# Expert weights in another order: second weights four rows to a partition, first weights read with a stride

## The chip, the cores and the metric

The kernel runs on one core of one Trainium2 chip. The metric is the device time of one execution in microseconds (us). The kernel before takes 616.64 us, the median of 9 runs between 615.38 and 618.8 us. The numbers on single instructions come from one profiled execution, which took 621.12 us.

## What is computed

Two transformer layers on `x` of 8 x 512 x 128 values in 32-bit floating point. Layer 0 is an attention with linear state plus a mixture of 8 experts of one matrix each. Layer 1 is an attention with a local window and latents plus a mixture of 8 experts with two matrices each. The part that the change touches is the expert layer of layer 1:

```python
logits = x_flat @ gate_w.T
probs = jax.nn.softmax(logits / TEMPERATURE, axis=-1)
topk_probs, topk_idx = jax.lax.top_k(probs, TOPK)          # 2 of 8
hidden = jax.nn.relu(jnp.einsum('th,ehf->tef', x_flat, w1) + b1[None])
all_out = jnp.einsum('tef,efh->teh', hidden, w2) + b2[None]
gathered = jnp.take_along_axis(all_out, topk_idx[:, :, None], axis=1)
y_flat = jnp.sum(gathered * topk_probs[:, :, None], axis=1)
```

`w1` is 8 x 128 x 512 and `w2` is 8 x 512 x 128. The kernel computes only the two chosen experts of each token. The sum over the 512 hidden units in the second product may be taken in any order, so long as both matrices and the bias `b1` agree on which unit is which.

## The kernel before

The 8 sequences form three groups of 2, 3 and 3. After layer 0, each group goes through `route` (L1152), `experts1` (L1309) and, in parallel with it, `attention1` (L923); `output` (L1431) adds the two. `route` sorts the tokens of a group by expert into tiles of 128 rows, so that each tile has one expert: 85 tiles in all.

For each tile, `fetch` (L1316) issues three loads on the queue of SyncE (SP): `load_first` (L1336), the first weights of the tile's expert, 128 partitions of 512 values; `load_second` (L1340), the second weights, with the hidden unit `k*128 + p` on partition p, block k; and `load_third` (L1344), the output bias spread over the partitions. Loads run three tiles ahead, in 3 buffers of first weights, 4 of second weights and 4 of bias. The expert's number is read into SP's registers (L1323). On TensorE (PE), `hp` (L1405 to 1410) is then made by four products of 128x128 by 128x128, one for each block k of 128 hidden units; the block of first weights is the stationary operand (it is loaded into the array), the tokens are the moving one. ScalarE (ACT) applies bias and relu into `ht`, and four more products add up into `yp` (L1420 to 1425), with `ht` stationary and the block k of second weights moving. In the profile each 32-bit product is two weight loads (PEld) and two matmuls (PE).

The first bias `b1` comes with the packed weights as columns. At the start it is transposed into `b1r` (L608 to 610): 32 rows of 128 values, row `4*e + k` holding the units of block k of expert e. `route` picks rows out of it by a product with a one-hot matrix `ohk` (L1226 to 1233), built from two constants that say which expert (`part4`, L109) and which block (`chunk4`, L110) a row of `b1r` belongs to. Its result is the tile's bias, used by the relu of L1414.

The order of all instructions is not written by hand. A recorder (L126) keeps every operation with its engine and an estimated time (`_duration`), and `order` (L238) lays them out with a list scheduler, by readiness and by the ranks of a table `PLAN` (L1461). The instructions are then emitted in that order, and each engine runs its own in that order. Operations recorded that way all show the line 389 in the profile; only the loads of `fetch` and the scatter L1371 have lines of their own. For a matmul, the estimate looks at the shapes of the operands and not at their strides. Where the plan has PE idle, `_fill` (L349) puts matmuls on zeros. SP's queue carries, besides the expert weights, the store of each sequence's layer-0 gates to memory (`gd`), the loads that spread them over the partitions (`gbc`, L704), the token rows, and the final reads and stores.

Of the kernel before, what the change touches and what calls it, by code (L numbers as in the profile page):

```python
# [10 lines left out]
F32 = mybir.dt.float32  # L11
# [8 lines left out]
P = 128  # L20
# [3 lines left out]
E = 8  # L24
FF = 512
NFC = FF // P
# [11 lines left out]
def _tiles(n):  # L38
    return (2 * n * N + E * (P - 1)) // P
# [34 lines left out]
def _constants():  # L74

    c = np.zeros((P, _CN), np.float32)
    p = np.arange(P)

    def put(name, a):
        lo, hi = _CCOL[name]  # L80
        c[: a.shape[0], lo:hi] = a.reshape(a.shape[0], hi - lo)

    put("ident", np.eye(P))

    less = np.eye(P)
    less[P - 1] = -1.0
    less[:, P - 1] = 0.0
    put("less", less)
    put("heads", p[:, None] // D == p[None, :] // D)
    put("head4", (p[:, None] // D) % 4 == np.arange(4)[None, :])  # L90
    put("head8", (p % LC)[:, None] // D == np.arange(LH)[None, :])

    i = np.arange(W)[None, :]
    put("seen_q", i <= p[:, None] % W)
    put("seen_k", p[:, None] % W <= i)
    put("past_k", p[:, None] % W > i)

    g = np.arange(P // CHUNK)
    late = np.zeros((P, P), np.float32)
    group = np.zeros((P, P), np.float32)  # L100
    for at in (0, LC):
        late[at : at + len(g)] = np.where(p[None, :] % len(g) > g[:, None], NEG, 0.0)
        group[at : at + len(g)] = p[None, :] // CHUNK == g[:, None]
    put("late", late)
    put("group", group)
    put("first", np.broadcast_to(E - np.arange(E), (P, NT, E)))
    put("before", p[:, None] < p[None, :])
    put("iota", np.broadcast_to(p, (P, P)))
    put("part4", p[:, None] // NFC)  # L109
    put("chunk4", p[:, None] % NFC == np.arange(NFC)[None, :])  # L110
    put("within", p)
    n = 2 * max(GROUPS) * NT
    put("tile", np.broadcast_to(1 + np.arange(n), (P, n)))
    return c
# [321 lines left out]
def two_layers_kernel(  # L436
# [14 lines left out]
    nc = Recorder(tc.nc)  # L451
# [5 lines left out]
    work = ctx.enter_context(tc.tile_pool(name="work", bufs=2))  # L457
    small = ctx.enter_context(tc.tile_pool(name="small", bufs=2))
    dram = ctx.enter_context(tc.tile_pool(name="dram", bufs=4, space=DRAM))
# [52 lines left out]
    def wt(name):  # L512
        lo, hi = _WCOL[name]
        return wsb[:, lo:hi]
# [62 lines left out]
    nc.gpsimd.memset(vb, 0.0)  # L577


    b1r = const.tile([E * NFC, P], F32, name="b1r")  # L580

    def mm(o, lhsT, rhs, start=True, stop=True):
        nc.tensor.matmul(o, lhsT, rhs, start=start, stop=stop)

    def bank(name, parts=P):
        t = ps.tile([parts, 512], F32, tag="bank", name=name)
        nc.banks[t[:].tensor.name] = t[:]
        return t
# [18 lines left out]
    less_last(wk0, wsb[:, lo : lo + kq], bias_row("k"), "k0", plus=3)  # L607
    b1p = bank("b1p")  # L608
    nc.tensor.transpose(b1p[: E * NFC, :P], wt("b1"), ident)
    nc.scalar.copy(b1r, b1p[: E * NFC, :P])  # L610

    def layernorm(dst, src, name, n=C):

# [695 lines left out]
    def experts1(h):  # L1309

        nm = f"_{h}"
        TILES = _tiles(GROUPS[h])
        row_i, token_i, _, bias, own_i = places[h]
        ws, xgs, xts, hts, numbers = {}, {}, {}, {}, {}

        def fetch(j):  # L1316

            if j % QUAD == 0:
                n = min(QUAD, TILES - j)
                number = own_i[0:1, j : j + n]  # L1320

                def load(q=j // QUAD):
                    _, numbers[q] = tc.nc.values_load_multi_w_load_instructions(  # L1323
                        number, engines=(mybir.EngineType.SP,), min_val=0, max_val=E - 1,
                        skip_runtime_bounds_check_because="a count of experts, held under E on the chip",
                    )

                nc.add("SP", load, [], [number], 1.5, 0.0)
                fetch.last = nc.ops[-1]
            first = work.tile([P, FF], F32, tag="w1", name=f"w1{nm}_{j}", bufs=3)  # L1330
            second = work.tile([P, NFC, C], F32, tag="w2", name=f"w2{nm}_{j}", bufs=4)
            third = work.tile([P, C], F32, tag="b2", name=f"b2{nm}_{j}", bufs=4)

            def load_first():
                e = bass.ds(numbers[j // QUAD][j % QUAD], 1)
                tc.nc.sync.dma_start(first, w1[e].rearrange("e p f -> (e p) f"))  # L1336

            def load_second():
                e = bass.ds(numbers[j // QUAD][j % QUAD], 1)
                tc.nc.sync.dma_start(second, w2[e].rearrange("e (k p) c -> p (e k) c", p=P))  # L1340

            def load_third():
                e = bass.ds(numbers[j // QUAD][j % QUAD], 1)
                tc.nc.sync.dma_start(third, experts_b[e, 1].to_broadcast([P, C]))  # L1344

            for move, to in ((load_first, first), (load_second, second), (load_third, third)):
                nc.add("SP", move, [to], [], 0.55, 3.3)
                nc.ops[-1].follows = (fetch.last,)
            ws[j] = first, second, third

        def gather(q):
            js = range(q * QUAD, min((q + 1) * QUAD, TILES))
            if not len(js):
                return
            xg = work.tile([P, QUAD, C], F32, tag="xgt", name=f"xgt{nm}_{q}", bufs=2)
            for a, j in enumerate(js):
                nc.gpsimd.indirect_dma_start(
                    xg[:, a], None, x_rows[h],
                    bass.IndirectOffsetOnAxis(ap=token_i[:, j : j + 1], axis=0),
                )  # L1360
            xgs[q] = xg

        views = dram_disjoint_views(y_rows[h], TILES)
        scattered[h] = []

        def scatter(j, ys):

            ids = row_i[:, j : j + 1]

            def store():  # L1370
                tc.nc.gpsimd.indirect_dma_start(  # L1371
                    views[j], bass.IndirectOffsetOnAxis(ap=ids, axis=0), ys, None
                )

            nc.add("POOL", store, [], [ys, ids], 1.25, 2.4)
            scattered[h].append(nc.ops[-1])

        def turn(q):
            if q not in xgs:
                return  # L1380
            xg = xgs.pop(q)
            n = min(QUAD, TILES - q * QUAD)
            tp = bank(f"tpx{nm}_{q}")
            for a in range(n):
                nc.tensor.transpose(tp[:, a * P : (a + 1) * P], xg[:, a], ident)
            xt = work.tile([P, QUAD * P], F32, tag="xt", name=f"xt{nm}_{q}", bufs=2)
            nc.scalar.copy(xt[:, : n * P], tp[:, : n * P])
            xts[q] = xt

        for j in range(AHEAD):  # L1390
            fetch(j)
        gather(0)
        yield
        turn(0)
        gather(1)
        yield
        for j in range(TILES + 1):
            if j < TILES:
                if j + AHEAD < TILES:
                    fetch(j + AHEAD)  # L1400
                q, a = divmod(j, QUAD)
                if a == 1:
                    turn(q + 1)
                    gather(q + 2)
                hp = bank(f"hp{nm}_{j}")  # L1405
                for k in range(NFC):
                    mm(
                        hp[:, k * P : (k + 1) * P], ws[j][0][:, k * P : (k + 1) * P],
                        xts[q][:, a * P : (a + 1) * P],
                    )  # L1410
                ht = work.tile([P, NFC, P], F32, tag="ht", name=f"ht{nm}_{j}", bufs=2)
                for k in range(NFC):
                    nc.scalar.activation(
                        ht[:, k], hp[:, k * P : (k + 1) * P], AF.Relu, bias=bias[:, k, j : j + 1]  # L1414
                    )
                hts[j] = ht
                yield
            if j:
                ht, (_, w2k, b2) = hts.pop(j - 1), ws.pop(j - 1)
                yp = bank(f"yp{nm}_{j - 1}")  # L1420
                for k in range(NFC):
                    mm(
                        yp[:, :C], ht[:, k], w2k[:, k],
                        start=k == 0, stop=k == NFC - 1,
                    )
                ys = work.tile([P, C], F32, tag="ys", name=f"ys{nm}_{j - 1}", bufs=YS)
                nc.vector.tensor_add(ys, yp[:, :C], b2)
                scatter(j - 1, ys)
                yield
# [49 lines left out]
    def put(name, stage, arg, at):  # L1479
        nc.begin(*PLAN[name][at])  # L1480
        for _ in stage(arg):
            pass
# [73 lines left out]
```

## Time and profile before

| what | value |
|---|---|
| median of 9 runs | 616.64 us |
| profiled execution | 621.12 us, of which 619.1 us from first to last instruction |
| mean granted TensorE clock | 0.961 of full speed |
| experts' first product, weight loads | 680, mean 194 ns, 186 at least |
| experts' first product, matmuls | 680, mean 280 ns, from 131.1 us to 579.7 us of the span |
| loads of second weights (L1340) | 85, issue 384 ns in the median |
| loads of first weights (L1336) | 85, issue 333 ns in the median |
| DMA queue of SP and ACT (q1) | 100,582 packets, 78.41 MB, 43.9% of 16 engines' span |

The span is the time from the first to the last instruction; the 2 us that the execution lasts beyond it are the start and the end around it. "Busy" is the time in which an engine has an instruction under way. Matmuls are pipelined: one of 275 ns overlaps the next, so the distance from start to start, not the duration, tells what a matmul costs in a row of matmuls. PEld is the loading of the stationary operand, which goes on beside the matmul of the operand loaded before.

### The profile page before, as it was taken

The page shows a single profiled execution, that of the slowest core. Times are in us where ns is not written, and L with a number is a line of the kernel's source. Part 1 is how long each engine was busy: PE and PEld are TensorE (multiplying, and loading weights), DVE is VectorE, ACT ScalarE, POOL GpSimd, SP SyncE. Part 2 cuts the span into 40 slices and gives each one's busy share as a digit, 9 for nine tenths or more (in the row PEclk, how much of TensorE's full clock was granted, in tenths as well). Part 3 has the DMA queues.
Part 4 walks back from the last instruction along what each step waited for, and adds up shares of the span by engine and source line. Part 5 has one row for each costly group of instructions (what it writes and reads, how often), then busy time and mean ns, then how long its engine had stood idle before and what let it go on. Part 6 is the DMA issues. An engine that isn't in the chain of part 4 may idle for free.

```text
span 619.1 us, 15660 instructions
## 1 busy us (share of the span) xinstructions
PE 550.7 (89%) x5487; PEld 453.9 (73%) x5487; DVE 477.0 (77%) x1297; ACT 342.7 (55%) x950; POOL 403.4 (65%) x422
## 2 busy tenths in 40 slices
PE   9999988889989899869998979988998899999873
PEld 3567766669778678758897867987777788888832
DVE  2396899988979889998867867789844784965695
ACT  2532746761864784536577347464485567557610
POOL 3015323679748837864777877887778888887562
PEclk8799999978999999999998889989999999999996
DMA  5035142554442334636654466666956767796222
GB/s 158 1 115 143 52 128 74 152 143 133 116 132 78 107 112 130 138 68 181 186 164 140 138 188 209 175 176 193 254 179 194 226 207 232 208 264 200 71 86 69
DMA packets 106532, 91.63 MB, mean 148 GB/s; under 512 B 8940, under 2 KB 84086, under 8 KB 106454
## 3 DMA queue, kind: packets, MB, share of 16 engines
q1 hardware_dynamic: 100582, 78.41, 43.9%
q0 software_dynamic: 5440, 11.15, 7.0%
q10 hardware_dynamic: 432, 1.07, 0.5%
q8 instruction: 44, 0.72, 0.5%
q14 instruction: 34, 0.28, 0.2%
HBM read 80.70 MB, written 9.90 MB: 146 GB/s over the span
## 4 chain that ended last, share of the span: by engine, by line
DVE 33%; PE 27%; POOL 15%; issue 8%; ACT 8%; DMA 8%; SPq 0%; DVEq 0%; POOLq 0%; ACTq 0%
PE rp L389 4%; POOL m L389 4%; PE hp L389 4%; DVE pw L389 4%; PE yp L389 3%; POOL y_rows L1371 3%; DMA gbc<-gd 3%; PE pv L389 3%; POOL xgt L389 2%; POOL pw L389 2%; ACT vb L389 2%; DVE m L389 2%; DMA xgt<-x_rows,token_i 2%; DVE xg L389 2%; DVE x L389 2%
## 5 line engine op out<-in xcount | busy, mean ns | idle before, releaser
L389 ACT ACTIVATE ht<-hp,bias 128x128 f32<-128x128 f32 x340 | 101.2, 372 | 44.8 <-PE hp L389 44.5
L1371 POOL DMA_INDIRECT y_rows<-ys,row_i x85 | 89.4, 1052 | 42.4 <-issue 9.7
L389 POOL DMA_INDIRECT xgt<-x_rows,token_i x85 | 87.2, 1026 | 23.0 <-issue 17.3
L389 PEld LDWEIGHTS hp<-xt,w 128*128 128x128 f32 x680 | 84.2, 194 | 12.8 <-issue 5.3
L389 PE MATMUL hp<-xt,w 128*128 128x128 f32 x680 | 91.7, 280 | 2.0 <-DVE ys L389 1.0
L389 PE MATMUL yp<-w,ht 128*128 128x128 f32 x680 | 90.6, 278 | 1.4 <-ACT ht L389 1.4
L389 PEld LDWEIGHTS yp<-w,ht 128*128 128x128 f32 x680 | 83.1, 192 | 6.6 <-ACT ht L389 3.0
L389 PE MATMUL rp<-we_sb,xg 128*128 128x128 f32 x512 | 68.2, 281 | 6.0 <-POOL xg L389 3.7
L389 POOL TENSOR_TENSOR xg<-xT,gbc 128x512 f32<-128x512 f32 x32 | 43.2, 1350 | 43.9 <-DMA gbc<-gd 31.3
L389 PEld LDWEIGHTS rp<-we_sb,xg 128*128 128x128 f32 x512 | 62.7, 195 | 11.8 <-POOL xg L389 6.5
L389 PE MATMUL pv<-pw,vb 128*32 128x64 f32 (+1 forms) x1088 | 37.9, 229 | 18.2 <-POOL pw L389 13.0
L389 PEld LDWEIGHTS pv<-pw,vb 128*32 128x32 f32 x1088 | 34.4, 119 | 25.3 <-POOL pw L389 22.1
L389 ACT ACTIVATE m<-m,zero_b 128x512 f32<-128x512 f32 x32 | 23.1, 723 | 39.6 <-POOL m L389 39.4
L389 POOL TENSOR_TENSOR pw<-pt,csb 128x512 f32<-128x512 f32 x32 | 42.3, 1323 | 3.6 <-DVE pt L389 3.3
L389 POOL TENSOR_TENSOR m<-m,ard 128x512 f32<-128x512 f32 x32 | 34.1, 1066 | 12.0 <-DVE ard L389 5.1
L389 DVE TENSOR_TENSOR pw<-pt,csb 128x512 f32<-128x512 f32 x32 | 40.5, 1267 | 0.3
L389 POOL TENSOR_TENSOR m<-m,amx 128x512 f32<-128x512 f32 x32 | 33.8, 1065 | 10.7 <-DVE amx L389 9.8
L389 POOL TENSOR_TENSOR le<-le,lrd 128x128 f32<-128x128 f32 (+3 forms) x32 | 23.9, 753 | 25.9 <-DVE lrd L389 18.7
L389 ACT COPY vb<-v 32x128 f32<-32x128 f32 x128 | 37.7, 295 | 1.8
L389 DVE COPY_PREDICATED m<-csb,sc 128x256 f32<-128x256 int32 x64 | 25.3, 435 | 15.3 <-POOL m L389 12.0
L389 PE MATMUL sc<-kT,qe 32*128 32x64 f32 x1024 | 36.0, 277 | 1.0 <-DVE k L389 0.6
L389 PEld LDWEIGHTS sc<-kT,qe 32*128 32x128 f32 x1024 | 33.0, 190 | 4.4 <-DVE k L389 1.1
(261 smaller groups left out, 1221.0 us busy)
## 6 DMA issues: line engine op xcount, KB each, us to landing
w<-in_w_dram SPq DMA_DIRECT2D x170, 256.0 KB
gbc<-gd SPq DMA_DIRECT2D x64, 256.0 KB
b<-in_experts_b_dram SPq DMA_DIRECT2D x85, 64.0 KB
yg<-y_rows SPq DMA_DIRECT2D x16, 256.0 KB
x<-in_x_dram SPq DMA_DIRECT2D x8, 256.0 KB
x_rows<-xn SPq DMA_DIRECT2D x8, 256.0 KB
out_dram<-x SPq DMA_DIRECT2D x8, 256.0 KB
xgt<-x_rows,token_i POOLq DMA_INDIRECT x85
```

Of the source, the lines that this page charges most:

```text
L389: r.ENGINES[name], lambda: call(*args, **kwargs), aps[:1], aps[1:], time, delay, shape
L1371: tc.nc.gpsimd.indirect_dma_start(views[j], bass.IndirectOffsetOnAxis(ap=ids, axis=0), ys, None)
```

## The change

The second weights are laid out so that partition p holds the hidden units `4*p` to `4*p + 3`. These four rows of `w2` lie next to each other in memory, so that one partition's data is one piece of 2 KB, where it was four pieces of 512 bytes. Block k is then the units `4*p + k`, so the first product takes, for block k, every fourth column of the first weights, beginning with k: a stride of 16 bytes in the stationary operand. The bytes moved are the same, and so are the number and shape of the products.

The bias has to follow. `b1r` now has the row `8*k + e`, holding the units `4*p + k` of expert e. At the start the transposed bias goes to a temporary tile `b1t`, from there by a store of 16 KB to a scratch in memory `b1d`, and comes back by four loads of 8 rows of 128 single values each (every fourth value). The two constants `part4` and `chunk4` are changed to the new row order. The five added DMAs are issued on SP's queue.

```diff
-    put("part4", p[:, None] // NFC)
-    put("chunk4", p[:, None] % NFC == np.arange(NFC)[None, :])
+    put("part4", p[:, None] % E)
+    put("chunk4", p[:, None] // E == np.arange(NFC)[None, :])
...
     nc.tensor.transpose(b1p[: E * NFC, :P], wt("b1"), ident)
-    nc.scalar.copy(b1r, b1p[: E * NFC, :P])
+    b1t = work.tile([E * NFC, P], F32, tag="pt", name="b1t", bufs=1)
+    nc.scalar.copy(b1t, b1p[: E * NFC, :P])
+    b1d = dram.tile([E, FF], F32, tag="b1d", name="b1d", bufs=1)
+    nc.sync.dma_start(b1d.rearrange("e (c p) -> (e c) p", p=P), b1t)
+    for k in range(NFC):
+        nc.sync.dma_start(
+            b1r[k * E : (k + 1) * E], b1d.rearrange("e (p k) -> k e p", k=NFC)[k]
+        )
...
-                tc.nc.sync.dma_start(second, w2[e].rearrange("e (k p) c -> p (e k) c", p=P))
+                tc.nc.sync.dma_start(second, w2[e].rearrange("e (p k) c -> p (e k) c", k=NFC))
...
                     mm(
-                        hp[:, k * P : (k + 1) * P], ws[j][0][:, k * P : (k + 1) * P],
+                        hp[:, k * P : (k + 1) * P], ws[j][0][:, k::NFC],
                         xts[q][:, a * P : (a + 1) * P],
                     )
```

## The prediction

> **What bounds the kernel now.** I read the page's busy shares first, then the chain that ended last, then the windows of the expert stage, all instructions and `hp` alone.
>
> ```profile
> PE 550.7 (89%) x5487; PEld 453.9 (73%) x5487; DVE 477.0 (77%) x1297; ACT 342.7 (55%) x950; POOL 403.4 (65%) x422
> ...
> DVE 33%; PE 27%; POOL 15%; issue 8%; ACT 8%; DMA 8%; SPq 0%; DVEq 0%; POOLq 0%; ACTq 0%
> PE rp L389 4%; POOL m L389 4%; PE hp L389 4%; DVE pw L389 4%; PE yp L389 3%; POOL y_rows L1371 3%; DMA gbc<-gd 3%; PE pv L389 3%; POOL xgt L389 2%; POOL pw L389 2%; ACT vb L389 2%; DVE m L389 2%; DMA xgt<-x_rows,token_i 2%; DVE xg L389 2%; DVE x L389 2%
> ```
>
> PE is the fullest engine, but the chain passes from one engine to another: PE holds 27% of it, and `hp` alone 3.6% (the chain's own view gives the tenths), 22.3 us of 619.1. DMA holds 8%, and the weights hardly appear. In the waits, PE and PEld wait for the weights `w` 1.6 us in all. SP's queue waits far longer for PE to free weight buffers (64.4 us at L1340) than anyone waits for the loads. So the transfer that the change improves is hidden now, and the weight load that it alters is on the fullest engine.
>
> The windows from 130 to 582 us, where all 680 passes of `hp` lie (a pass is one weight load with its matmul). Columns: stretch and its length, PE busy (count), PEld busy (count); in the second view of `hp` alone.
>
> ```profile
> 130.00:200.00 70.00, 63.49 (x667) 54.37 (x666) 60.49 (x157) 39.19 (x104) 53.58 (x53) 0.98 0.45 129
> 200.00:290.00 90.00, 78.90 (x848) 65.25 (x849) 84.40 (x241) 57.20 (x152) 58.03 (x58) 1.00 0.43 114
> ...
> 430.00:500.00 70.00, 63.70 (x639) 53.77 (x638) 46.34 (x122) 41.26 (x127) 56.65 (x60) 1.00 0.73 210
> 500.00:582.00 82.00, 78.20 (x913) 69.81 (x912) 52.39 (x120) 54.57 (x172) 63.83 (x66) 1.00 0.73 208
> ```
>
> ```profile
> 130.00:200.00 70.00, 6.36 (x48) 5.83 (x48) 7.26 (x24) 0.98 0.45 129
> 200.00:290.00 90.00, 11.72 (x88) 10.92 (x88) 12.81 (x42) 1.00 0.43 114
> ...
> 430.00:500.00 70.00, 20.32 (x152) 18.53 (x152) 21.48 (x75) 1.00 0.73 210
> 500.00:582.00 82.00, 24.57 (x184) 22.63 (x184) 27.93 (x98) 1.00 0.73 208
> ```
>
> PE is idle there for 6.5, 11.1, 4.2, 8.1, 6.3 and 3.8 us (the two stretches left out have 72 and 136 passes): 40 us of 452, and least where `hp` is densest.
>
> **Part 1, the strided weight load.** First, what sets the pace of a pass. The timeline of PEld at 98.6 us shows weight loads beside short matmuls; that of 340 us shows one tile's `hp`:
>
> ```profile
> 98.64 0.30 PEld L389 LDWEIGHTS cp<-m,csb 128*128 128x128 f32 x2
> 98.86 0.30 PEld L389 LDWEIGHTS tot<-m,ones 128*128 128x128 f32 x2
> 99.08 0.30 PEld L389 LDWEIGHTS wgp<-wgl,wqT 128*128 128x128 f32 x2
> ```
>
> ```profile
> 340.09 0.97 PEld L389 LDWEIGHTS hp<-xt,w 128*128 128x128 f32 x8
> ```
>
> `cp` and `tot` have matmuls of only 64 moving columns, and still their loads follow each other at 0.22/2 = 110 ns. So a load of 128 columns in 32-bit takes 110 to 112 ns of the array's time by itself. `hp` runs at (0.97 - 0.19)/7 = 111 ns per pass; I use 112. A matmul of 128 columns needs nearly the same (the gate transposes `gp`, with a weight of 8 columns, follow at 109 ns in the trace's records). The two streams are level, so whatever the load loses, the pass loses: there is no slack to hide a slower load.
>
> No weight load of the trace has a stride; the memory patterns recorded for them are all contiguous. The bounds on a load with a stride of 16 bytes:
> - From below: 112 ns, no change. A gain is excluded, since the matmul holds the pass at 109 ns (at most 3 ns x 680 = 2 us).
> - From above: the 128 values now lie over 2,048 bytes of the partition, where they lay over 512. If the read had to walk the whole stretch at today's rate, 4 x 112 = 448 ns, +336 ns x 680 = 228 us.
> - Between: the fastest weight read of the trace is that of `ohr` in 16 bits, 256 bytes in (0.40 - 0.19)/7 = 30 ns (eight `inv` matmuls in 0.40 us, each 0.19). Walking 2,048 bytes at that rate takes 240 ns. I take a doubling, 224 ns: next to that row, and the geometric middle of 112 and 448. Extra: 112 ns x 680 = 76 us of PE time.
>
> [...]
>
> How much of 76 us reaches the end? By stage the extra is 48, 88, 72, 136, 152 and 184 passes x 0.112 = 5.4, 9.9, 8.1, 15.2, 17.0 and 20.6 us. Bounds: nothing absorbed, 76. The present chain lengthened only by its own `hp` pieces, doubled: 22. Between them, all of PE's idle time taken up stage by stage: 0 + 0 + 3.9 + 7.1 + 10.7 + 16.8 = 38.5. I take the middle of 22 and 76, 49 us. What is late next is ACT, which waits for `hp` already (44.5 us in 35 waits), then `ht`, `yp` and the scatter.
>
> **Part 2, second weights in pieces of 2 KB.** Per load 128 packets instead of 512, the same bytes. In the trace's packet records one of 512 bytes takes 28.8 ns in the mean (75,016 packets), one of 2,048 bytes 109.5 ns (median 84; 19,136 packets). On each of 16 engines a load goes from 32 x 28.8 = 0.92 us to 8 x 109.5 = 0.88, or 8 x 84 = 0.67 at best: 0.04 to 0.25 us less. PE waits for `w` 1.6 us in all, so the direct gain is at most that. Behind the loads in the queues, `gbc`, `xgt` and the bias land sooner; the chain has 8% = 50 us of landings in some 20 pieces, so at most 20 x 0.25 = 5 us. I take 1 us. SP's issue falls from 384 ns to the 333 of L1336, 4 us of an engine that is not on the chain: nothing.
>
> **Part 3, the bias at the start.** The copy on ACT (0.25 us) stays. The store is as large as `gd`'s (0.33 us issue; landing 1.45 us in the chain). Four loads of 1,024 single values: the trace's two loads of 128 single values took 0.55 us to issue against 0.28 for a plain one, 2.1 ns a value, so some 2.5 us each, and their packets 9 ns. On 8 engines 4,096 packets take 4.6 us, on one 37. From 16.7 us (copy done) this gives about 29 us for the issue. SP has nothing between 9.1 and 32.05 us (`gd`), and `b1r` is first read at 107.1 us: nothing, covered by that gap. If the cover fails, the gates of the first sequence come late by up to 25 us at the very worst (16.7 + 3 + 37 = 57 against 32); I keep 0 to 5. The wait that `bp` gains is long satisfied. `b1t` borrows a buffer whose next user starts at 119.2 us. The recorder's estimate sees no stride, so the order of the other engines should stay.
>
> **Sum.** Profiled execution: 621.1 + 49 - 1 = 669. The median of the runs is 4.5 us below the profiled one: 616.6 + 48 = 664.6, said as 665.
>
> **The rivals.**
> 1. The strided load is as fast as the contiguous one. For: nothing in the trace says that the array's own 112 ns isn't what bounds a load. Against: the 16-bit row shows that the array takes weights faster, so 112 is a rate of reading. Then only parts 2 and 3 remain: 616.6 - 1 = 615.6, between 611.6 and 617.8. This is the case on the other side: shorter landings of `gbc` and `xgt` behind the weight loads, at the end of the expert stage where DMA is busy 0.73, pay from the point at which the load costs under 1 us / 680 = 1.5 ns more.
> 2. A partial price, 1.2 to 1.6 times: 22 to 67 ns x 680 = 15 to 46 us of PE time, of which two thirds (49/76) arrive: 626 to 646.
> 3. The walk at today's rate, 448 ns: +228 us, less the idle 40: about 805.
>
> **How the numbers follow.** Doubled (638 to 692 by the bounds 22 and 76): 0.46. No price: 0.36. Partial: 0.13. Quadrupled: 0.03. A late start or a changed order that outweighs the rest: 0.02. The doubled case's own range is 638 to 692. With two cases so far apart, the range runs from within the free case to within the doubled one: 613.5 to 685; it leaves out some 0.05 of the free case, 0.06 of the doubled one and the 0.03. About 0.2% (1.2 us) is what a measurement of this kernel can tell from no change. Within the free case 615.4 is about the middle: faster 0.17, same 0.17, slower by the rest 0.66.
>
> **What would show it.** PEld rows of `hp`: mean near 300 ns instead of 194, eight of them over 1.7 us instead of 0.97; `yp` beside it unchanged at 192. PE idle in the windows after 350 us nearly gone. If the `hp` loads stay at 194, part 1 is wrong and the time is near 615.6. If they double and the time grows by under 22 us, the path was misread. The weights' packets should fall by 32,640, and SP's queue should stand free before `gd` at 32 us.

## The result, and the profile after

The changed kernel takes 648.25 us in the median (644.97 to 651.75, 15 runs), the kernel before beside it 616.51 us (46 runs). The ratio is 1.0516, 95% interval 1.0498 to 1.0534: 31.7 us slower. The profiled execution of the changed kernel has a span of 651.6 us.

The page of the changed kernel shows the busy shares, the chain that ended last by engine and by line, and the groups of the first product, of its relu and of the second product's weight loads:

```profile
PE 613.7 (94%) x5487; PEld 526.2 (81%) x5487; DVE 478.6 (73%) x1297; ACT 345.5 (53%) x950; POOL 402.7 (62%) x422
...
PE 67%; DVE 19%; POOL 4%; ACT 4%; DMA 3%; issue 2%; SPq 0%; DVEq 0%; POOLq 0%
PE hp L389 23%; PE yp L389 11%; PE rp L389 5%; PE pv L389 4%; PE sc L389 3%; PE kp L389 2%; PE rem_p L389 2%; PE gj L389 2%; DVE xg L389 2%; DVE pw L389 2%; DMA gbc<-gd 2%; PE sl L389 1%; POOL m L389 1%; DVE x L389 1%; PE tpx L389 1%
...
L389 PEld LDWEIGHTS hp<-xt,w 128*128 128x128 f32 x680 | 165.5, 327 | 8.7 <-issue 2.6
L389 PE MATMUL hp<-xt,w 128*128 128x128 f32 x680 | 171.0, 397 | 0.3 <-ACT gsb L389 0.3
L389 ACT ACTIVATE ht<-hp,bias 128x128 f32<-128x128 f32 x340 | 101.8, 368 | 98.7 <-PE hp L389 96.7
...
L389 PEld LDWEIGHTS yp<-w,ht 128*128 128x128 f32 x680 | 82.8, 192 | 4.1 <-issue 2.4
```

PE now holds 67% of the chain, where it held 27%, and `hp` alone 23%. The weight load of `hp` went from 194 to 327 ns in the mean; that of `yp`, which reads its block contiguously, stayed at 192. No other engine's busy time moved by more than 3 us. ACT's waits for `hp` doubled, from 44.5 to 96.7 us, but ACT has only 4% of the chain, and PE waits for its `ht` 0.5 us in all.

The windows of the changed kernel, columns as in the prediction, the last one 32 us longer because the experts end later:

```profile
130.00:200.00 70.00, 66.99 (x675) 58.92 (x674) 60.77 (x161) 39.72 (x104) 54.04 (x54) 1.00 0.46 130
200.00:290.00 90.00, 84.11 (x832) 72.55 (x831) 83.64 (x236) 56.21 (x149) 57.33 (x57) 1.00 0.40 111
...
430.00:500.00 70.00, 69.81 (x542) 64.00 (x541) 42.07 (x119) 36.87 (x114) 51.07 (x53) 1.00 0.64 182
500.00:614.00 114.00, 114.00 (x1107) 105.96 (x1106) 63.27 (x146) 62.72 (x192) 76.22 (x77) 1.00 0.64 177
```

From 430 us on PE is idle for 0.2 us in all (70 - 69.81, then 114 - 114.00); in the kernel before it was idle for 6.3 and 3.8 us in the last two windows. The pace of a pass is read from the timeline of PEld, two tiles in a row:

```profile
548.96 3.81 PEld L389 LDWEIGHTS hp<-xt,w 128*128 128x128 f32 x16
```

(3.81 - 0.33)/15 = 232 ns from load to load, where it was 111. In the trace's records the median is 233 ns against 111 to 112: about 121.5 ns more for each of 680 passes, 82.6 us of PE time. Of that, 31.7 us (38%) arrived. In both traces PE runs its 5,487 matmuls in the same order, so the difference does not come from another schedule. The open questions were two: whether the load alone is to blame, and where the other 51 us went.

### The profile page after: what moved, and what is told of

Its sections match the earlier page's. It is cut to its first block, busy times and chain, and to the rows that moved or that the text cites. A ratio compares the mean times of both kernels' runs of the same rounds, so it can differ in the third digit from the quotient of the medians.

```text
span 651.6 us, 15669 instructions
## 1 busy us (share of the span) xinstructions
PE 613.7 (94%) x5487; PEld 526.2 (81%) x5487; DVE 478.6 (73%) x1297; ACT 345.5 (53%) x950; POOL 402.7 (62%) x422
## 4 chain that ended last, share of the span: by engine, by line
PE 67%; DVE 19%; POOL 4%; ACT 4%; DMA 3%; issue 2%; SPq 0%; DVEq 0%; POOLq 0%
PE hp L389 23%; PE yp L389 11%; PE rp L389 5%; PE pv L389 4%; PE sc L389 3%; PE kp L389 2%; PE rem_p L389 2%; PE gj L389 2%; DVE xg L389 2%; DVE pw L389 2%; DMA gbc<-gd 2%; PE sl L389 1%; POOL m L389 1%; DVE x L389 1%; PE tpx L389 1%
## 5 line engine op out<-in xcount | busy, mean ns | idle before, releaser
L389 PEld LDWEIGHTS hp<-xt,w 128*128 128x128 f32 x680 | 165.5, 327 | 8.7 <-issue 2.6
L389 PE MATMUL hp<-xt,w 128*128 128x128 f32 x680 | 171.0, 397 | 0.3 <-ACT gsb L389 0.3
L389 ACT ACTIVATE ht<-hp,bias 128x128 f32<-128x128 f32 x340 | 101.8, 368 | 98.7 <-PE hp L389 96.7
L389 PE MATMUL yp<-w,ht 128*128 128x128 f32 x680 | 89.0, 276 | 0.0
L389 DVE TENSOR_TENSOR ys<-yp,b 128x128 f32<-128x128 f32 x85 | 24.0, 283 | 37.7 <-PE yp L389 37.4
L389 PEld LDWEIGHTS pv<-pw,vb 128*32 128x32 f32 x1088 | 31.2, 112 | 14.2 <-POOL pw L389 10.5
L389 PE MATMUL pv<-pw,vb 128*32 128x64 f32 (+1 forms) x1088 | 34.6, 219 | 8.1 <-POOL pw L389 5.6
```

The costliest lines, as they stand in the source:

```text
L389: r.ENGINES[name], lambda: call(*args, **kwargs), aps[:1], aps[1:], time, delay, shape
```

## The experiments

All runs but the last one below (the second dose) were made on a chip on which the kernel before takes about 642 us; so each run is compared with the kernel before of its own series, and times are given as ratios. In the runs marked with "columns" the products take other columns than the reference's, as the expectations say; the work is of the same size.

**Theory 1**: the strided weight load is the whole cause, and packets and bias detour cost and bring nothing. **Rival**: one of these has a part in the loss.

### Stride alone (columns)

```diff
-                        hp[:, k * P : (k + 1) * P], ws[j][0][:, k * P : (k + 1) * P],
+                        hp[:, k * P : (k + 1) * P], ws[j][0][:, k::NFC],
```

The edit is made in the kernel before.

> The kernel before with one edit: the first weights are read with the stride of 16 bytes; second weights and bias stay in the old order, so the hidden units of the two products do not agree (that part of the computation is changed). Theory 1, the strided weight load is the whole cause: the changed kernel's time, 649 us (647 to 651), hp loads of 329 ns. Rival, the new layout of the second weights or the bias detour has a part in the loss: at most 640 us.

Measured: ratio 1.051 (1.044 to 1.058), the changed kernel's 1.0516 within its interval; 674.09 us on that chip, so the absolute time of the expectation does not apply. The loads have a median of 329 ns. The stride alone gives the whole loss.

### Everything but the stride (columns)

```diff
-                        hp[:, k * P : (k + 1) * P], ws[j][0][:, k::NFC],
+                        hp[:, k * P : (k + 1) * P], ws[j][0][:, k * P : (k + 1) * P],
```

The edit is made in the changed kernel.

> The changed kernel with the first weights read in contiguous blocks again; 2 KB pieces of second weights and the bias detour stay, so the hidden units of the two products do not agree (that part is changed). Theory 1: the kernel before less what the bigger packets bring, 615.5 us (613.5 to 617). Rival, packets or detour cost by themselves: 620 us or more.

Measured: ratio 1.0009 (0.9976 to 1.0043). The rival falls. The loads have a median of 192 ns again. Packets of 2 KB and the detour together change nothing that can be measured; a gain of over 0.24% is excluded. Two things in the traces fit this: PE waited for the weights 1.6 us in all, and the bigger packets are hardly faster (in the changed kernel 30,016 packets of 2,048 bytes take 109.6 ns in the mean, four of 512 bytes took 4 x 28.8 = 115). The run doesn't tell the two apart.

### Two rows to a partition: stride of 8 bytes

```diff
-                tc.nc.sync.dma_start(second, w2[e].rearrange("e (p k) c -> p (e k) c", k=NFC))
+                tc.nc.sync.dma_start(second.rearrange("p (h d) c -> p h (d c)", d=2), w2[e].rearrange("e (h p d) c -> p (e h) (d c)", h=2, d=2))
...
-                        hp[:, k * P : (k + 1) * P], ws[j][0][:, k::NFC],
+                        hp[:, k * P : (k + 1) * P], ws[j][0][:, k // 2 * 2 * P + k % 2 : k // 2 * 2 * P + 2 * P : 2],
```

The edit is made in the changed kernel. The bias detour is rearranged in the same way (not shown), so both products agree on the units.

> Two rows of second weights to a piece of 1 KB, so the first weights are read with a stride of 8 bytes. Theory 1a, the load slows only when no two neighbours lie within 16 bytes: loads of 192 ns, time 616 us (614 to 617.5). Theory 1b, the price grows with the stretch walked (16 bytes cost 122 ns a pass, 8 bytes a third of the way from 1 to 4, 40 ns, 27 us of PE time): loads near 235 ns, time 624 to 632 us.

Measured: ratio 1.0024 (0.9987 to 1.0062); loads of 196 ns, 118 ns from load to load instead of 112. Nearly theory 1a: a stride of 8 bytes costs 6 ns a pass and not 40. No gain shows in it either.

### Strides of 1, 2, 3 and 4 in one kernel (columns)

```diff
-                hp = bank(f"hp{nm}_{j}")
+                step = 1 + j % 4
+                hp = bank(f"hp{'abcd'[j % 4]}{nm}_{j}")
...
-                        hp[:, k * P : (k + 1) * P], ws[j][0][:, k * P : (k + 1) * P],
+                        hp[:, k * P : (k + 1) * P], ws[j][0][:, k * (P if step == 1 else 1) :][:, : step * (P - 1) + 1 : step],
```

> The kernel before with strides of 1, 2, 3 and 4 values in the first weights of every fourth tile (hpa, hpb, hpc, hpd); the first product takes other columns than it should in three tiles of four. Theory 1a (two values within 16 bytes suffice): loads of 192, 192, then 192 to 260 for 12 bytes, and 329 ns. Theory 1b (price grows with the stretch): 192, 235, 280 and 329 ns. Time between before and after, 620 to 632 us.

The loads by tile (columns: count, then shortest, median and longest duration in ns, then first and last start):

```profile
L389 PEld LDWEIGHTS hpa<-xt,w x176: 186/192/333, 127.3 to 596.0; 128*128 128x128 f32 x176
...
L389 PEld LDWEIGHTS hpb<-xt,w x176: 193/197/332, 128.9 to 598.1; 128*128 128x128 f32 x176
...
L389 PEld LDWEIGHTS hpc<-xt,w x176: 251/262/333, 132.6 to 602.7; 128*128 128x128 f32 x176
...
L389 PEld LDWEIGHTS hpd<-xt,w x152: 308/329/332, 148.0 to 591.2; 128*128 128x128 f32 x152
```

The medians are 192, 197, 262 and 329 ns, and the paces in the records 112, 118, 174 and 233 ns. Neither theory gave all four: 8 bytes are almost free (1a), but from there on the pace grows by 56 to 59 ns for each value of stride (1b). Two readings remain: a fixed price per piece of 16 bytes touched (64, 96 and 128 pieces at strides 2, 3 and 4: 1.84, 1.81 and 1.82 ns a piece), or a price per byte of the stretch walked. The kernel was run once: 643.37 us, against 642.12 in the median for the kernel before, below the 620 to 632 us of the expectation (0.6 to 2.5% over the kernel before) although the slower loads add some 30 us of PE time. One run has no interval, so this only hints at what "Where the rest of the 82.6 us went" tests.

### Strides of 4, 5, 6 and 8 (columns)

```diff
-                hp = bank(f"hp{nm}_{j}")
+                step = (4, 5, 6, 8)[j % 4]
+                hp = bank(f"hp{'abcd'[j % 4]}{nm}_{j}")
...
-                        hp[:, k * P : (k + 1) * P], ws[j][0][:, k * P : (k + 1) * P],
+                        hp[:, k * P : (k + 1) * P], we_sb.rearrange("p e c -> p (e c)")[:, k : k + step * (P - 1) + 1 : step],
```

> The kernel before, with the stationary operand of the first product taken out of the 1,024 columns of layer 0's expert weights at strides of 4, 5, 6 and 8 values (hpa, hpb, hpc, hpd by every fourth tile); the first product is therefore another one. Theory L, the price is one unit per piece of 16 bytes touched, and a stride over 16 bytes touches no more pieces than values: pitch 233 ns at 4, 5, 6 and 8 alike. Theory S, the price goes with the stretch of memory walked (8.8 bytes per ns, as strides 2, 3 and 4 have it): 233, 291, 350 and 466 ns.

```profile
L389 PEld LDWEIGHTS hpa<-xt,we_sb x176: 307/329/333, 130.8 to 625.8; 128*128 128x128 f32 x176
...
L389 PEld LDWEIGHTS hpb<-xt,we_sb x176: 294/314/338, 132.6 to 628.6; 128*128 128x128 f32 x176
...
L389 PEld LDWEIGHTS hpc<-xt,we_sb x176: 296/316/340, 137.1 to 634.1; 128*128 128x128 f32 x176
...
L389 PEld LDWEIGHTS hpd<-xt,we_sb x152: 312/334/338, 152.1 to 620.2; 128*128 128x128 f32 x152
```

The paces are 233, 220, 222 and 237 ns. Theory S (up to 466) falls and theory L holds within 6%: the times go with the pieces of 16 bytes that the load touches, 1.7 to 1.9 ns each, and from a stride of 16 bytes on it touches one piece per value and gets hardly worse (233 ns at 16 bytes, 237 at 32). Another size of piece does not fit: pieces of 8 bytes would make strides of 8 and 16 bytes alike, where 118 and 233 ns were measured, and pieces of 32 would make 32 bytes twice as dear as 16. That strides of 5 and 6 are 5% faster than 4 and 8 was not expected, and is left open.

### Where the rest of the 82.6 us went

**Theory A**: PE's own waiting swallowed it, so that the first part of the extra work is cheap and the last is paid in full. **Theory B**: a constant share, 39% as I put it, arrives, as of any work of which a part lies on the chain.

In the changed kernel, with `early` as `h < 2`, `late` as `h == 2` and `half` as `j % 2` (columns in all three):

```diff
-                        hp[:, k * P : (k + 1) * P], ws[j][0][:, k::NFC],
+                        hp[:, k * P : (k + 1) * P], (ws[j][0][:, k::NFC] if early else ws[j][0][:, k * P : (k + 1) * P]),
```

> The changed kernel with the strided load only in the first two groups (54 tiles, 432 passes); the third group reads contiguous blocks, so its two products disagree on the hidden units (that part is changed). Extra weight-load time 432 x 0.1215 = 52.5 us. Theory A, the extra is paid out of the time in which TensorE would have waited anyway, and little of that is left at the end: of the 5.1% this carries 1.2 to 2.4%, ratio to the kernel before 1.012 to 1.024. Theory B, a constant share (39%) of the extra arrives wherever it lies: 1.032.

> The changed kernel with the strided load only in the third group (31 tiles, 248 passes); the first two groups read contiguous blocks, so their two products disagree on the hidden units (that part is changed). Extra 248 x 0.1215 = 30.1 us. Theory A: most of it arrives, ratio 1.025 to 1.035, more than from the early groups although the extra is smaller. Theory B: 1.018.

> The changed kernel with the strided load in every second tile (41 of 85, 328 passes); the other tiles read contiguous blocks, so their two products disagree on the hidden units (that part is changed). Extra 39.9 us, spread evenly. Theory A, the first part of an even extra is nearly free and the last part costs in full: ratio 1.004 to 1.016, less than half of 1.051. Theory B: half of it, 1.025.

| where the stride is | extra on PE | ratio to before, interval | A | B |
|---|---|---|---|---|
| groups 1 and 2 | 52.5 us | 1.0273, 1.0218 to 1.0329 | 1.012 to 1.024 | 1.032 |
| group 3 | 30.1 us | 1.0237, 1.0171 to 1.0302 | 1.025 to 1.035 | 1.018 |
| every second tile | 39.9 us | 1.0103, 1.0039 to 1.0166 | 1.004 to 1.016 | 1.025 |

The two runs by group lie between the theories and decide nothing: the measured ratios miss both forecasts of A and both of B, and the intervals touch all four. The two parts add up (2.73% + 2.37% = 5.10%, the whole loss), so there is no sign that slack of one group pays for work in another. The third run decides. Half of the extra, spread evenly, costs 1.0%, a fifth of the whole loss, and B's 1.025 is outside its interval. The second half costs the other four fifths. The traces of this chip fit theory A: while the experts run, PE is idle for 53 us without the stride (128 to 606 us), for 31 with it in every second tile (129 to 614) and for 19 with the stride alone (127 to 637). The first half of the extra takes up more idle time than the second.

### A second dose

```diff
-                        yp[:, :C], ht[:, k], w2k[:, k],
+                        yp[:, :C], ht.rearrange("p k t -> p (k t)")[:, k::NFC], w2k[:, k],
```

The edit is made in the changed kernel (columns).

> The changed kernel with the stationary operand of the second product (ht) read at a stride of 16 bytes too, so that its columns are not those the second product should take (that part is changed). Another 680 x 0.1215 = 82.6 us of weight loads on top of the first 82.6. Theory A, the waiting time of TensorE that swallowed most of the first dose is used up: at least 65 us of the second dose arrive, ratio to the kernel before 1.15 to 1.19. Theory B, a constant share of 39%: ratio 1.10.

Measured: ratio 1.1691 (1.1614 to 1.1769), 720.3 us against 616.18 us of the kernel before in that series. The chain, the weight loads of `yp` and the whole expert stretch of this kernel:

```profile
PE 75%; DVE 13%; POOL 5%; DMA 2%; issue 2%; ACT 2%; SPq 0%; POOLq 0%; DVEq 0%
PE yp L389 21%; PE hp L389 21%; PE rp L389 5%; PE pv L389 4%; PE sc L389 3%; PE rem_p L389 2%; PE kp L389 2%; PE gj L389 2%; DMA gbc<-gd 2%; PE sl L389 2%; POOL xgt L389 1%; POOL m L389 1%; PE fp L389 1%; DVE pw L389 1%; POOL xg L389 1%
...
L389 PEld LDWEIGHTS yp<-w,ht 128*128 128x128 f32 x680 | 165.4, 328 | 3.2 <-issue 1.5
```

```profile
131.00:685.00 554.00, 547.40 (x4426) 508.15 (x4428) 350.62 (x907) 273.75 (x777) 337.13 (x341) 1.00 0.47 134
```

The first 82.6 us cost 31.7 us, the second 104.1 - 31.7 = 72 us, 88%. Theory A holds, B (1.10) falls. With this edit each block of `yp` also reads columns of all four relus and so depends on all of them; but the trace has no wait for `ht` in front of `yp`, so the extra time is that of the loads. PE is idle for 6.6 us of 554 here. The same view of the kernel before and of the changed kernel:

```profile
131.00:580.00 449.00, 409.05 (x4418) 356.44 (x4418) 349.30 (x903) 271.29 (x783) 337.91 (x340) 0.98 0.59 169
```

```profile
131.00:614.00 483.00, 471.93 (x4417) 429.05 (x4415) 350.62 (x907) 274.73 (x784) 339.08 (x342) 1.00 0.56 157
```

PE's idle time in the stretch fell from 40 to 11 us, 29 of the 51 that did not arrive. PE's busy time grew by only 63 us for 82.6 us of extra work. Two things can account for that, and both are argued, not shown. A matmul counts as busy for 275 ns, of which only 112 were its pace, so gaps under 163 ns between passes were counted as busy, and the extra may have filled some of them too. And the clock changed: in the trace's clock records the spells at half speed that begin within the stretch, 3.4 us each, are five before (from 140 us on) and one after, so that up to 4 x 1.7 = 7 us may have come back. No run here separates the two.

## Why the prediction was right or wrong

- **The sign, the range and the mechanism** held: the load and the matmul of a pass were level (111 against 109 ns), so the slower load set the pace (233 ns). 648.25 us lies between 613.5 and 685; but that range was drawn to hold the free load as well, so that it held says little. The doubled load was the likeliest case (0.46), and it is what came. The single value, 665 us, was 17 us too high.
- **The price of the load** held: 224 ns expected, 233 measured, 82.6 us where 76 were summed. In part this was luck: 224 was a choice between 112 and 448, and no row of the kernel before showed a strided load. The kept trace could not have shown one, for the strided `hp` loads of the changed kernel are recorded with the same memory pattern as the contiguous ones; that no load before had a stride rests on the kernel's text. The row that the choice stood next to, the 16-bit weight read of `ohr`, agrees in size with the price per piece (256 bytes in 30 ns are 16 pieces at 1.9 ns). That this is the same cost is not shown: its matmuls have only 62 columns, and the row does not tell whether they or the loads set the 30 ns.
- **The share that arrives** is the step that was wrong: "I take the middle of 22 and 76, 49 us". 31.7 us came, 17 us less, below even the 38.5 us of the sum by stages (44 with the measured 121.5 ns a pass). Nothing in the profile stood behind a middle. The sum by stages was the better ground: PE's idle time took up 29 us, and the first half of an even extra was cheap. Why it was still too high is in part open; it took the idle time from PE's busy column, which does not show gaps shorter than a matmul's tail (163 ns for `hp`: 275 busy at a pace of 112), and it kept the clock as it was. The total lay between the lower end, the chain lengthened by its own `hp` pieces (22), and the upper end.
- **"What is late next is ACT"** was wrong. ACT waits longer for `hp` (96.7 us) but holds 4% of the chain; what is late is PE itself, with 67% of it.
- **Part 2**: 1 us was taken, and the run without the stride shows -0.24% to +0.43%. It fits, and so does nothing at all. That "the transfer that the change improves is hidden now" agrees with it, but is not tested by it, since the bigger packets made the transfer hardly shorter (109.6 ns for 2,048 bytes where it was 115).
- **Part 3** held. The four loads took 0.76 to 1.90 us to issue and ended at 23.0 us, sooner than the 29 expected; `gd` was issued at 31.90 us, where it had been at 32.05:

```profile
16.58 0.34 SPq L389 DMA_DIRECT2D b1d<-b1t  x1
18.04 5.00 SPq L389 DMA_DIRECT2D b1r<-b1d  x4
31.90 0.28 SPq L389 DMA_DIRECT2D gd<-gT  x1
```

- **The rivals**: a free load is refuted by the loads of 329 ns; a partial price of 174 ns a pass exists, but at a stride of 12 bytes; a changed order is refuted by PE's unchanged one; the walk at the contiguous rate (448 ns) is refuted by the 233 ns measured.

## What to carry to other kernels

A stride in the stationary operand is not free because it is only an access pattern: read first from the trace whether the load or the matmul sets the pace of a pass (here 111 against 109 ns), for where they are level, a slower load slows every pass (233 ns where it was 112). Here up to 8 bytes of stride passed for little (1.0024, 0.9987 to 1.0062), and from 16 bytes on the pace was about doubled (220 to 237 ns against 112). A new layout for a transfer that PE hardly waited for (1.6 us) gave nothing that could be measured (1.0009). Extra work on the fullest engine cost little at first (1.0% for the first half, spread evenly) and nearly all of it later (88% of the second dose): do not scale a loss by a share, but count the idle time of that engine where the work lies, and remember that its busy time can hide short gaps (here those under 163 ns).

## What was not expected of the hardware

A 32-bit weight load of 128 columns took 1.7 to 1.9 ns for each piece of 16 bytes that it touched in a partition, with 112 ns as the least: 118, 174 and 233 ns from load to load at strides of 8, 12 and 16 bytes, 220 and 222 at 20 and 24, 237 at 32. A DMA of 8 rows of 128 single values cost little in packets (11 ns each in the records, 9 in the median) and more in its issue: 0.76 to 1.90 us for 1,024 values, where the store of the same 32 rows in one piece per row took 0.34.
